# Layer 3's feed-forward weights prepared inside layer 2's feed-forward loop

## The chip, the cores and the metric

One core of a Trainium2 chip runs the whole program. The metric is the device time of one execution in microseconds (us); less is better. Five runs of the kernel before gave a median of 2343.83 us (2341.57 to 2348.78).

## What is computed

Four layers work on x (4 batches of 256 tokens of 256 numbers), each with an attention over a context of 1601 tokens and a feed-forward part. Two pieces of the reference matter here. Layer 2's feed-forward part chooses one of 4 experts for each token; layer 3's rounds its three weight matrices to -1, 0 or 1 by the mean of their absolute values:

```python
def _L2_ffn_ref(...):                      # 4 experts, top 1
    g = jnp.einsum('td,edf->tef', x, Wg)   # D_FF = 1024
    u = jnp.einsum('td,edf->tef', x, Wu)
    y = jnp.einsum('tef,efd->ted', jax.nn.silu(g) * u, Wd)
...
def _quant_weight(w):                      # layer 3: w_gate, w_up, w_down
    scale = jnp.mean(jnp.abs(w)) + EPS
    wq = jnp.clip(jnp.round(w / scale), -1.0, 1.0)
    return (wq, scale)
```

Each of the three matrices is 256 x 1024 in float32, 1 MB. Nothing in them depends on x, so they can be prepared at any time before layer 3's first feed-forward product.

## The kernel before, in words

**Layer 2's feed-forward part** is `l2_ffn` (L988). Tokens are sorted by expert into 11 groups of 128; the sorted rows are fetched with indirect DMAs on GpSimd's queue (`f2xr`, L1134). The loop at L1183 has 44 working steps (4 chunks of the hidden width times 11 groups) and two more. In a step, TensorE makes `f2gu` of one group, turns the `f2h` of the step before, and multiplies the `f2h` of two steps before into `f2y`; ScalarE takes the silu and copies `f2hT`; VectorE multiplies into `f2h` (L1158) and adds `f2y` into `f2acc` (L1176). Steps 10 to 15 also carry one piece each of layer 3's early keys and values (`fill`, L1188), the last of which ends in a root of `ss` and in `l3_spread` (L1841): GpSimd scales `kr` (L1850) and makes the lower halves (L1901), VectorE makes the upper halves (L1900) and turns them into `kt` (L1854), SyncE sends `kt` to a buffer `kd` in DRAM. The instructions of this function are placed by a scheduler, except those that are pinned to the order in which they were written (`pin`, L165).

**Layer 3** is `l3` (L1917). Its main loop has 208 steps: 4 batches, 4 passes over the context in each, 13 steps of 128 context tokens in a pass. A step makes eight score products `s`, two exponentials `e` of 128 x 1024 on ScalarE, and, for the step before, eight products into `o`. After a pass, VectorE copies `o` to `os` (L2308); the tile `o` has one buffer, so the next pass's products into `o` wait for that copy. Keys come back from `kd` as `kf` through SyncE's queue (L2123) and GpSimd copies them to `kb` (L2132).

Everything else of layer 3 is laid into these steps as streams of pieces: `slot` (L2216) lets one piece that needs TensorE into a step, and others by their stated VectorE cost until some 2 us are full. In batch 0 the streams are the weights (`weights`, L2006), the next batches' keys (`l3_keys`), their spreading (`l3_spreads`), and the next batch's queries and values. In this loop all instructions stand in the order in which they were written, on every engine.

`weights` handles the matrices one after the other, each in two halves of 128 x 1024: two loads on GpSimd's queue, two sums of absolute values on VectorE (`wsum`), a product with a matrix of ones on TensorE that adds them over the partitions, three small operations for the scale, and three VectorE operations for each half (multiply and round by adding a large number; subtract it and cut above; cut below into bfloat16). Layer 3's feed-forward pieces (`half`, L2209) start in batch 1 and wait until all three are there.

Of the kernel before, what the change touches and what calls it, by code (L numbers as in the profile page):

```python
# [11 lines left out]
F32 = mybir.dt.float32  # L12
BF16 = mybir.dt.bfloat16
# [11 lines left out]
P = 128  # L25
# [3 lines left out]
D = 256  # L29
# [68 lines left out]
class Kernel:  # L98
# [889 lines left out]
    def l2_ffn(self, other):  # L988
# [13 lines left out]
        with ExitStack() as es:  # L1002
# [142 lines left out]
            def brought(n):  # L1145
                tp = ps.tile([P, 2, P], F32, name="f2tpx", tag="tp")
                for k in range(2):
                    nc.tensor.transpose(tp[:, k, :], xr[n][:, k * P : (k + 1) * P], self.ident)
                self.evac(xsT[:, n], tp)
                expert.append(nc.tensor.value_load(ei[:, n : n + 1], min_val=0, max_val=E2 - 1))  # L1150
# [28 lines left out]

            work = [(c, n) for c in range(NC) for n in range(NS)]  # L1180
            hs, hTs = {}, {}
            brought(0)
            for s in range(len(work) + 2):  # L1183
                if s < len(work):
                    hs[s] = gated(*work[s])
                    if s + 1 < NS:
                        brought(s + 1)
                    elif s < NS + 5:  # L1188
                        fill(1)
                    elif s >= len(work) - 5:  # L1190
                        fill(1)
                if 0 <= s - 1 < len(work):
                    hTs[s - 1] = turned(hs.pop(s - 1))
                if s >= 2:
                    down(*work[s - 2], hTs.pop(s - 2))
                    c, n = work[s - 2]
                    if n == NS - 1 and c + 2 < NC:
                        chunks.append(load(c + 2))
            self.back = []
            for t in range(8):  # L1200
                if t % 4 == 0:
# [546 lines left out]
    def values3(self, pool):  # L1748
# [6 lines left out]
            self.nc.vector.memset(t[:, :, n:], 1.0)  # L1755
        return va

    def l3_begin(self, b, st):
        st["kr"] = self.a3.tile([P, NM, D], F32, name="kr3")
        st["ss"] = self.a3.tile([P, NM * NH3], F32, name="ss3")  # L1760
        st["kd"] = self.dram.tile([16, 32, MP], F32, name=f"kd3{b}")
        st["made"] = 0
# [154 lines left out]
    def l3(self, first):  # L1917
# [10 lines left out]
        with ExitStack() as es:  # L1928
# [5 lines left out]
            ps_o = es.enter_context(tc.tile_pool(name="a3o", bufs=1, space=PSUM))  # L1934
            idb = self.idb
            self.va3.append(self.values3(self.late3))
            wq, ws = {}, {}

            def bank():
                return ps.tile([P, 512], F32, name="b3", tag="tp")  # L1940
# [25 lines left out]
            def queries(b, st, fill=lambda n: None):  # L1966
# [35 lines left out]
                fill(2)  # L2002
                st["qr"] = qr
                yield 0.0

            def weights():  # L2006

                for name, n in (("l3_wg", 2), ("l3_wu", 2), ("l3_wd", 8)):
                    v = i[name].rearrange("(k p) e -> p k e", p=P)
                    w = []  # L2010
                    for c in range(2):
                        w.append(two.tile([P, I3], F32, name="wf3", tag="g3"))
                        nc.gpsimd.dma_start(
                            w[c].rearrange("p (k e) -> p k e", k=n // 2), v[:, c * n // 2 : (c + 1) * n // 2]
                        )
                    for _ in range(2):
                        yield 0.0
                    sm = self.small.tile([P, 2], F32, name="wsum")
                    for c in range(2):
                        yield 1.2  # L2020
                        nc.vector.tensor_reduce(sm[:, c : c + 1], w[c], AX.X, ALU.add, apply_absolute_value=True)
                    yield 0.0
                    yield True
                    tot = bank()[:, 0:2]
                    self.mm(tot, self.ones, sm, True, True)
                    s = one.tile([P, 1], F32, name=name + "s")
                    r = self.small.tile([P, 1], F32, name="wrec")
                    nc.vector.tensor_reduce(s, tot, AX.X, ALU.add)
                    nc.vector.tensor_scalar(s, s, 1.0 / (I3 * D), 1e-5, ALU.mult, ALU.add)
                    nc.vector.reciprocal(r, s)  # L2030
                    wb = one.tile([P, n, 2048 // n], BF16, name=name + "b")
                    wr = wb.rearrange("p k e -> p (k e)")
                    for c in range(2):
                        yield 0.8
                        nc.vector.tensor_scalar(w[c], w[c], r, RND, ALU.mult, ALU.add)
                        yield 0.7
                        nc.vector.tensor_scalar(w[c], w[c], RND, 1.0, ALU.subtract, ALU.min)
                        yield 0.7
                        nc.vector.tensor_scalar(wr[:, c * I3 : (c + 1) * I3], w[c], -1.0, None, ALU.max)
                    wq[name], ws[name] = wb, s  # L2040
                    yield 0.0

            def scale_of(v, name):

# [162 lines left out]
                states[b]["xn"] = normed(b, rs[:, b, :])  # L2207

            def half(b, q):  # L2209
                while len(wq) < 3 or "xn" not in states[b]:  # L2210
                    yield 0.0
                yield 0.7
                yield from ffn(b, q, states[b]["xn"], lambda dt: ps.tile(
                    [P, 512 if dt is F32 else 1024], dt, name="b3", tag="tp"))
# [47 lines left out]
            self.clock3 = 0  # L2262
            for at, (b, g, c) in enumerate(order):
                if g + c == 0:
                    streams = [t for t in streams if t.left] if b else [Stream(weights(), 3)]
                    st = states[b + 1] if b + 1 < B else None
                    if b + 1 < B:
                        every.n, every.share = 0, K3[b]
                        if b == 0:
                            streams += [every, Stream(self.l3_spreads(states), 1)]  # L2270
                if c == 0:
                    o = ps_o.tile([P, 2 * S], F32, name="o3")
                    now_q = q
                k, m0 = k1, PARTS[c][0]
                for m in range(*PARTS[c]):
                    e = scores(k, now_q, (m, m0))
                    if m == m0 and at + 1 < len(order):
                        k1 = exact(*kf)
                        if at + 2 < len(order):
                            b1, g1, c1 = order[at + 2]  # L2280
                            while "sent" not in states[b1]:
                                slot(streams, True, 2.0)
                            kf = keys(b1, g1, *PARTS[c1])
                    free = True
                    if m == 2 and done is not None:
                        close(*done)
                        done = None
                        free = False
                    if m == 7 and (g < 3 or b + 1 < B):
                        b1, g1 = (b, g + 1) if g < 3 else (b + 1, 0)  # L2290
                        while "qr" not in states[b1]:
                            slot(streams, True, 2.0)
                        ask = asked(b1, g1)
                        q = next(ask)
                    if m == 9 and (g < 3 or b + 1 < B):
                        next(ask)
                        free = False
                    if g * NM + m == 1 and b + 1 < B:
                        asking, valuing = Stream(ahead(b + 1, st), 2), Stream(self.l3_values(b + 1, st), 13 if b else 2)
                        streams += [asking, valuing]  # L2300
                    if g * NM + m == 3 and b:
                        streams += [Stream(behind(b - 1), 1), *(Stream(half(b - 1, n), 7) for n in range(2))]
                    slot(streams, free, 1.7 - (0.6 if m == 0 else 0.0) - (0.0 if free else 0.9))
                    if last is not None:
                        values(*last)
                        if last[4] == NM - 1:
                            os = one.tile([P, 2 * S], F32, name="os3")
                            nc.vector.tensor_copy(os, last[1])  # L2308
                            done = (last[5], os, last[3])
                    last = (e, o, states[b]["va"], g, m, b)  # L2310
                if (g, c) == (3, len(PARTS) - 1):
                    due = streams if b + 1 == B else [asking, valuing]
                    while any(t.left for t in due):
                        slot(streams, True, 2.0)
# [19 lines left out]
    def run(self):  # L2334
# [21 lines left out]
            self.l1_ffn(weights)  # L2356
        self.l2_xattn()
        with ExitStack() as es:
            self.l3_open(es)
            first = {}  # L2360
            kv = self.l3_early(0, first, lambda: True)
            self.l2_ffn(kv)
            self.l3(first)
# [124 lines left out]
```

## Time and profile before

| what | value |
|---|---|
| median of five runs | 2343.83 us |
| the profiled execution | 2350.39 us |
| its span | 2348.7 us |
| TensorE busy | 2244.7 us (96%) |
| VectorE busy | 1478.0 us (63%) |
| ScalarE busy | 1277.9 us (54%) |
| layer 2's feed-forward loop, first to last silu | 1693.5 to 1826.7 us |
| layer 3's steps, first to last exponential | from 1855.9 us to about 2313 us |

PE is TensorE's matrix products, DVE is VectorE, ACT is ScalarE, POOL is GpSimd, SP is SyncE. Times in views of the trace are microseconds from the start of the span. L117 and L77 are the lines of two helpers through which many operations are recorded, so tiles are named beside them. The chain of waits follows the work that ended last back from step to step. The clock is the share of TensorE's full clock that was granted.

### The profile page before, as it was taken

The page shows a single profiled execution, that of the slowest core. Times are in us where ns is not written, and L with a number is a line of the kernel's source. Part 1 is how long each engine was busy: PE and PEld are TensorE (multiplying, and loading weights), DVE is VectorE, ACT ScalarE, POOL GpSimd, SP SyncE. Part 2 cuts the span into 40 slices and gives each one's busy share as a digit, 9 for nine tenths or more (in the row PEclk, how much of TensorE's full clock was granted, in tenths as well). Part 3 has the DMA queues.
Part 4 walks back from the last instruction along what each step waited for, and adds up shares of the span by engine and source line. Part 5 has one row for each costly group of instructions (what it writes and reads, how often), then busy time and mean ns, then how long its engine had stood idle before and what let it go on. Part 6 is the DMA issues. An engine that isn't in the chain of part 4 may idle for free.

```text
span 2348.7 us, 42217 instructions
## 1 busy us (share of the span) xinstructions
PE 2244.7 (96%) x14322; PEld 1383.7 (59%) x14335; DVE 1478.0 (63%) x3553; ACT 1277.9 (54%) x2877; POOL 951.6 (41%) x1707
## 2 busy tenths in 40 slices
PE   8989999999989999999999999999899989999996
PEld 5677978867745565556565555656666533443332
DVE  5543645943567777777777777777344574757344
ACT  3334546633665555554455555553232587888994
POOL 2014655512445455445554455544120354334220
PEclk9989999989999999999999999999899999999998
DMA  7165687733721111111111111100543453434320
GB/s 271 42 187 166 185 155 211 259 97 108 229 80 39 45 52 52 52 52 52 52 35 51 43 52 52 52 10 1 213 137 108 142 144 101 101 94 107 82 64 17
DMA packets 156078, 234.47 MB, mean 100 GB/s; under 512 B 33929, under 2 KB 122761, under 8 KB 154666
## 3 DMA queue, kind: packets, MB, share of 16 engines
q1 hardware_dynamic: 138998, 190.07, 26.1%
q0 software_dynamic: 11280, 31.60, 6.0%
q10 hardware_dynamic: 5588, 10.09, 1.4%
q8 instruction: 117, 1.92, 0.3%
q14 instruction: 95, 0.78, 0.1%
HBM read 169.94 MB, written 61.74 MB: 99 GB/s over the span
## 4 chain that ended last, share of the span: by engine, by line
PE 76%; DVE 8%; DMA 5%; issue 4%; ACT 3%; POOL 3%; SPq 1%; ACTq 0%; POOLq 0%; DVEq 0%
PE o L117 18%; PE s L117 17%; PE o L77 6%; PE b L77 3%; PE f2gu L117 3%; PE s L77 3%; PE f1gu L117 3%; PE f0gu L117 2%; PE acc L117 2%; PE tpq L117 2%; PE av L117 2%; PE fill L1307 2%; DMA f0xr<-f0xd,f0src 2%; PE f0y L117 2%; PE f2y L117 1%
## 5 line engine op out<-in xcount | busy, mean ns | idle before, releaser
L1572 ACT ACTIVATE p<-s,nmsm 128x448 f32<-128x448 f32 (+2 forms) x512 | 324.3, 638 | 369.8 <-DVE nmsm L1567 313.4
L117 PE MATMUL o<-pT,va 128*128 128x256 f32 (+2 forms) x1920 | 434.1, 379 | 3.0 <-DVE pT L1613 2.8
L117 PE MATMUL s<-kT,qT 128*32 128x448 f32 (+2 forms) x4096 | 424.2, 551 | 4.2 <-ACT p L1572 4.2
L77 ACT ACTIVATE e<-s 128x1024 f32<-128x1024 f32 (+1 forms) x416 | 392.4, 1042 | 58.1 <-PE s L77 56.9
L117 PEld LDWEIGHTS o<-pT,va 128*128 128x128 f32 (+1 forms) x1920 | 346.7, 191 | 127.6 <-issue 75.4
L1607 POOL TENSOR_SCALAR p<-p,rm 128x448 f32<-128x448 f32 (+2 forms) x512 | 319.5, 645 | 6.3
L1567 DVE TENSOR_REDUCE nmsm<-s 128x1 f32<-128x448 f32 (+4 forms) x384 | 293.5, 784 | 4.4
L1613 DVE STREAM_TRANSPOSE pT<-p 128x448 f32<-128x448 f32 (+4 forms) x384 | 278.1, 780 | 10.7 <-POOL p L1607 10.7
L117 PEld LDWEIGHTS s<-kT,qT 128*32 128x32 f32 x4096 | 121.7, 110 | 250.5 <-issue 214.1
L77 PE MATMUL o<-e,va 128*32 128x512 f32 x1656 | 247.8, 616 | 12.7 <-DVE os L77 10.8
L1600 POOL TENSOR_TENSOR rm<-em,tot 32x8 f32<-32x8 f32 x256 | 49.9, 195 | 336.1 <-DVE tot L1597 303.8
L1564 DVE TENSOR_TENSOR s<-s,mask 128x64 f32<-128x64 f32 (+4 forms) x384 | 92.7, 260 | 129.0 <-PE s L117 82.9
L77 PEld LDWEIGHTS s<-qb,kb 32*128 32x128 f32 (+1 forms) x1664 | 65.9, 182 | 182.9 <-issue 145.1
L522 POOL DMA_INDIRECT f0xr<-f0xd,f0src x95 | 91.6, 964 | 60.9 <-PE f0tph L579 49.5
L1307 PE MATMUL fill<-wkc_early,ctxT 128*128 128x256 f32 (+1 forms) x444 | 109.5, 398 | 6.9 <-ACT va_early L1315 4.6
L77 PE MATMUL s<-qb,kb 32*128 32x256 f32 (+1 forms) x1664 | 112.0, 333 | 3.1 <-ACT e L77 1.8
L77 POOL CAST kb<-kf 128x384 fp32r<-128x384 f32 (+1 forms) x126 | 64.9, 544 | 102.6 <-PE s L77 61.6
L1572 ACT ACTIVATION_READ_ACCUMULATOR p<-s,nmsm 128x1 f32 x512 | 100.6, 196 | 0.0
L1307 PEld LDWEIGHTS fill<-wkc_early,ctxT 128*128 128x128 f32 (+1 forms) x444 | 86.2, 198 | 22.8 <-ACT va_early L1315 5.8
L77 PEld LDWEIGHTS o<-e,va 128*32 128x32 f32 x1656 | 40.8, 109 | 74.9 <-issue 37.3
L117 PE MATMUL f2gu<-f2wgu,f2xsT 128*128 x176 | 84.1, 602 | 0.8 <-issue 0.5
L630 POOL DMA_INDIRECT f0yt<-f0yd,f0slot x64 | 68.2, 1066 | 35.7 <-DMA kd<-kT_early 16.5
(579 smaller groups left out, 3678.7 us busy)
## 6 DMA issues: line engine op xcount, KB each, us to landing
kf<-kd SPq DMA_DIRECT2D x384, 48.0 KB
vd<-va_early SPq DMA_DIRECT2D x96, 128.0 KB
kd<-kT_early SPq DMA_DIRECT2D x48, 256.0 KB
kT<-kd SPq DMA_DIRECT2D x16, 768.0 KB
va<-vd SPq DMA_DIRECT2D x16, 768.0 KB
kd<-kt SPq DMA_DIRECT2D x96, 128.0 KB
f0yd<-f0ys SPq DMA_DIRECT2D x95, 128.0 KB
ctxT<-in_ctxT SPq DMA_DIRECT2D x5, 1664.0 KB
```

Source lines behind the costliest of these rows:

```text
L77: ins = f(*a, **kw)
L117: self.ordered(self.nc.tensor.matmul(out, lhsT, rhs, start=start, stop=stop, **kw))
L522: nc.gpsimd.indirect_dma_start(out=t, out_offset=None, in_=xd[:, :], in_offset=bass.IndirectOffsetOnAxis(ap=src[:, n : n + 1], axis=0),)
L630: nc.gpsimd.indirect_dma_start(out=yt, out_offset=None, in_=yd[:, :], in_offset=bass.IndirectOffsetOnAxis(ap=slot[:, t, r : r + 1], axis=0),)
L1307: ins = nc.tensor.matmul(tp[:rows, t, :], ctxT[u // NKV2][:, k, c0 : c0 + rows], w[u % NKV2][:, k, :], start=k == 0, stop=k == 1,)
L1564: nc.vector.tensor_tensor(sv, sv, mask[:, e0:e1, : nt - CT, :].rearrange("p n t i -> p n (t i)"), ALU.add)
L1567: nc.vector.tensor_reduce(ms[:, 0, e0:e1], s[:, n0:n1, : nt * 32], AX.X, ALU.max, negate=True)
L1572: nc.scalar.activation(p[:, n, : nt * 32], s[:, n, : nt * 32], AF.Exp, bias=ms[:, 0, e : e + 1], accum_out=ms[:, 1, e : e + 1],)
L1600: nc.gpsimd.tensor_tensor(r[32 * a : 32 * a + 32], e[:, a], tot, ALU.mult)
L1607: nc.gpsimd.tensor_scalar(p[:, n, : nt * 32], p[:, n, : nt * 32], r[:, e : e + 1], 1.0, ALU.mult, ALU.mult)
L1613: self.pin(nc.vector.transpose(pT[:, 2 * c + n0 : 2 * c + n1, :nt, :].rearrange("p n t i -> p n (t i)"), p[:, n0:n1, : nt * 32],))
```

## The change

A new generator `l3_weights` does what `weights` did, with tiles of its own, and layer 2's loop takes one piece of it at the end of each step from step 6 on. A piece is one sum, the product with its small operations, the first rounding operation, or the second and third together; three steps pass between the loads of a matrix and its first sum. The VectorE operations are pinned; the loads and the products are not. The stream `weights` leaves layer 3, and `half` waits no more for it.

```diff
@@ l2_ffn
             work = [(c, n) for c in range(NC) for n in range(NS)]
             hs, hTs = {}, {}
+            wf = es.enter_context(tc.tile_pool(name="f2wf", bufs=2))
+            small = self.l3_weights(wf, self.take)
             brought(0)
             for s in range(len(work) + 2):
...
+                if s >= 6:
+                    next(small, None)
+            for _ in small:
+                pass
@@ Kernel
+    def l3_weights(self, pool, bank):
+        nc = self.nc
+        self.wb3, self.ws3 = {}, {}
+        self.w3 = self.es3.enter_context(self.tc.tile_pool(name="w3", bufs=1, side="right"))
+        for name, n in (("l3_wg", 2), ("l3_wu", 2), ("l3_wd", 8)):
+            v = self.i[name].rearrange("(k p) e -> p k e", p=P)
+            w = []
+            for c in range(2):
+                w.append(pool.tile([P, I3], F32, name="wf3", bufs=2))
+                nc.gpsimd.dma_start(w[c].rearrange("p (k e) -> p k e", k=n // 2), v[:, c * n // 2 : (c + 1) * n // 2])
+            for _ in range(3):
+                yield
+            sm = self.small.tile([P, 2], F32, name="wsum")
+            for c in range(2):
+                self.pin(nc.vector.tensor_reduce(sm[:, c : c + 1], w[c], AX.X, ALU.add, apply_absolute_value=True))
+                yield
+            tot = bank()[:, 0:2]
+            self.ordered(nc.tensor.matmul(tot, self.ones, sm, start=True, stop=True))
+            s = self.ws3[name] = self.w3.tile([P, 1], F32, name=name + "s")
+            r = self.small.tile([P, 1], F32, name="wrec")
+            self.pin(nc.vector.tensor_reduce(s, tot, AX.X, ALU.add))
+            self.pin(nc.vector.tensor_scalar(s, s, 1.0 / (I3 * D), 1e-5, ALU.mult, ALU.add))
+            self.pin(nc.vector.reciprocal(r, s))
+            wb = self.wb3[name] = self.w3.tile([P, n, 2048 // n], BF16, name=name + "b")
+            wr = wb.rearrange("p k e -> p (k e)")
+            for c in range(2):
+                yield
+                self.pin(nc.vector.tensor_scalar(w[c], w[c], r, RND, ALU.mult, ALU.add))
+                yield
+                self.pin(nc.vector.tensor_scalar(w[c], w[c], RND, 1.0, ALU.subtract, ALU.min))
+                self.pin(nc.vector.tensor_scalar(wr[:, c * I3 : (c + 1) * I3], w[c], -1.0, None, ALU.max))
@@ l3
-            wq, ws = {}, {}
+            wq, ws = self.wb3, self.ws3
...
-            def weights():
...
             def half(b, q):
-                while len(wq) < 3 or "xn" not in states[b]:
+                while "xn" not in states[b]:
...
-                    streams = [t for t in streams if t.left] if b else [Stream(weights(), 3)]
+                    streams = [t for t in streams if t.left] if b else []
@@ run
         with ExitStack() as es:
+            self.es3 = es
             self.l3_open(es)
```

More of the change, by code (lines that the diff above doesn't have):

```diff
@@ L2004, in queries @@
                 yield 0.0
-            def weights():
[L2008 to L2041, printed above, removed]
             def scale_of(v, name):
```

## The prediction

> **What bounds the kernel now.** I read the busy shares by slice first, then layer 3 cut into its passes, the chain of waits at the places where a pass is too long, and at last the rows of the moved work. The first columns are 40 slices of 58.7 us.
>
> ```profile
> PE   8989999999989999999999999999899989999996
> DVE  5543645943567777777777777777344574757344
> ACT  3334546633665555554455555553232587888994
> ```
>
> TensorE is busy nearly everywhere. VectorE stands at 3 to 4 tenths in layer 2's feed-forward part (slices 29 to 31, counted from 1) and at 5 and 7 where layer 3 begins (slices 32 and 33). Next come windows whose edges I set where the exponentials of a pass begin: four passes of batch 0, then the first of batch 1. Columns: length, busy time and count of PE, weight loads, DVE, ACT and POOL, then the granted clock.
>
> ```profile
> 1856.00:1885.00 29.00, 27.99 (x218) 11.31 (x218) 23.57 (x62) 23.91 (x26) 11.14 (x18) 0.88 0.63 204
> 1885.00:1920.00 35.00, 28.83 (x234) 10.72 (x232) 27.51 (x60) 25.15 (x29) 17.64 (x23) 0.90 0.55 133
> 1920.00:1947.00 27.00, 25.91 (x227) 9.68 (x224) 11.24 (x25) 24.58 (x28) 11.39 (x21) 1.00 0.61 147
> 1947.00:1978.00 31.00, 30.07 (x252) 13.27 (x256) 15.89 (x42) 24.96 (x26) 11.66 (x18) 1.00 0.28 71
> 1978.00:2015.00 37.00, 33.09 (x264) 14.49 (x262) 23.28 (x57) 25.18 (x27) 16.83 (x24) 0.91 0.54 136
> ```
>
> Where nothing disturbs it a step lasts 1.84 us (18 exponentials take 16.52 us in the timeline), a pass 23.9. The second and the fifth window are 11 and 13 us too long, PE is idle 6 and 4 us in them, and the clock is below 1. The chain of waits between the first two passes names the cause (start, length, work):
>
> ```profile
> 1884.34 1.69 DVE xn L77 x2
> 1886.03 1.48 DVE l_wgb L77
> 1887.52 1.16 DVE kt L77
> 1888.67 0.64 DVE wf L77
> 1889.31 0.60 DVE xT L77
> 1889.90 0.60 DVE wf L77
> 1890.51 0.61 DVE os L77
> ```
>
> VectorE is behind with its pieces, `os` stands at the end of its queue, and the next pass's products into `o` wait for `os`. Three of these rows are weights.
>
> **What the change moves.**
>
> ```profile
> L77 DVE TENSOR_REDUCE wsum<-wf x6: 1189/1210/1219, 1867.6 to 1934.5; 128x1 f32<-128x1024 f32 x6
> L77 DVE TENSOR_SCALAR wf<-wf,wrec x6: 705/743/1077, 1880.2 to 1974.8; 128x1024 f32<-128x1024 f32 x6
> L77 DVE TENSOR_SCALAR wf<-wf x6: 677/683/686, 1883.4 to 1979.1; 128x1024 f32<-128x1024 f32 x6
> L77 DVE TENSOR_SCALAR l_wgb<-wf x2: 684/1123/1562, 1886.0 to 1891.4; 128x1024 bf16<-128x1024 f32 x2
> L77 POOL DMA_DIRECT2D wf<-in_l_wg x2: 563/578/593, 1857.5 to 1858.1; - x2
> ```
>
> (ns: least, median, most.) On VectorE the `wf` tiles cost 22.1 us in 24 operations, and nine small ones of some 0.16 us make 23.5. On TensorE three products with ones cost 0.26 plus 0.19 for the weights. On GpSimd six load issues cost 3.9 us. All of it goes from layer 3 into layer 2's loop; the total on each engine stays the same.
>
> *Gain 1, passes 1 and 2 (64 us).* In the changed order of VectorE, with this trace's mean durations, the work ahead of the first `os` falls from 29.0 to 25.3 us and from there to the second from 25.0 to 17.5: 54.0 against 42.8. So VectorE is no longer the limit, and ScalarE's floor of 47.8 us (26 steps) is. Above it remain what the weights don't cause: the slow steps at the start (two of 4.7 and 3.1 us with the clock at half: 4), a few query and key products (1), and perhaps half of the boundary stall (3), since other pieces move up into the freed room. 56 against 64: **8 us**. Ends: 2.7, the three rows of the chain alone; 11.2, all of the VectorE work.
>
> *Gain 2, passes 3 and 4 (58 us).* The 13 key products of batch 2 begin in pass 3 instead of late in it, since the spreading is through earlier. Each makes a step 2.5 us (PE `s` 0.44, `b` 1.06, `o` 1.00) wherever it stands: twice 23.9, plus 13 times 0.66, is 56.4. **1 us**; ends -2 and 3.
>
> *Gain 3, the boundary to batch 1 (37 us).* There the chain runs POOL `sq`, DVE `ss`, DVE `l_wdb`, DVE `os`, PE `o` (1.93 us at half clock instead of 1.00). In the changed order only short root operations precede that `os`. **3 us**; ends 0.6, the `l_wdb` row alone, and 6, the whole stall with the slow clock behind it.
>
> A rule on the clock bears here: the trace shows half clock granted right after each of these stalls, about 3.4 us at a time (0.90 over 35 us is the same loss). [...]
>
> *Cost 1, the start of layer 2's loop.* In the changed order GpSimd issues the first load before the gathers `f2xr` that TensorE waits for (PE is idle from 1684.4 to 1689.2). The issue is 0.6 us, and its 512 KB share the software queue with the gathers: 1.2 us at the 426 GB/s that the DMA view shows at most. They overlap in part; **1.2 us**, ends 0.5 and 2.5.
>
> *Cost 2, three products with ones* stand on TensorE, which has no gap in that loop (69.8 of 70 us busy from 1760). 0.45 each: **1.3 us**; ends 0.6 (weight loads hidden) and 1.4. In layer 3 they are within gains 1 and 2.
>
> *Cost 3, the wait in the middle of the loop.* Today `kt` on VectorE waits for GpSimd's `kr` and `half` (POOL fills the chain from 1747.2 to 1757.0 except 0.8 us), `f2h` waits behind `kt`, and two steps are 1.2 and 2.0 us late. In the changed order GpSimd does six `kr` (6.6 us) and a load issue before the first `half`, where it did three, so the first `kt` comes 4 us later; but one more `f2h` stands ahead of it, and a step is 2.8 us. A sum of 1.2 stands ahead of the next `f2h`. With the 1.7 us for which VectorE sits idle before each `f2h` as slack, I count 3.5 us of stall instead of 3.2: **0.3 us**; ends -3.2 (gone) and 4.
>
> *Cost 4, the pieces themselves.* The largest is 0.68 + 0.7 us in the 1.7 us of idle time of a step: **0**. That cover fails where an operation of 0.7 takes 1.6, as the `l_wgb` row has it while GpSimd works; then a step is some 0.6 late, and three or four such make the other end, 2.
>
> [...]
>
> *At nothing:* the four memsets of `va` (0.9 us) move behind the loop, where VectorE waits from 1830 to 1836 for `f2yt`; without that cover, 1 us. `kt` is sent to `kd` some steps later, on a queue that finished 20 us ahead of layer 3.
>
> **Sum:** 8 + 1 + 3 - 1.2 - 1.3 - 0.3 = 9.2 us less. The profiled execution took 2350.39 us (span 2348.7), 6.6 above the median of 2343.83 and near the highest run; the gain is a difference within it, so I take it off the median: **2334.6 us**.
>
> **The rivals.**
>
> *More comes free* (0.20). All three gains near their upper ends, since each stall brings slow clock with it: 11 + 2 + 5 - 2 = 16 less, 2328. For it: window two has 6 us of idle PE. Against it: the freed room fills with other VectorE pieces.
>
> *Hidden anyway* (0.16). The passes are held by GpSimd and by the way of the keys through `kd`, so that only the rows on the chains go: 2.7 + 0 + 0.6 - 1.2 = 2 less, 2342. For it: POOL `sq` and `half` stand on the chains. That the weights keep work in layer 3 is excluded by the order: no piece of them is left there.
>
> *Slower: the loop waits for the loads* (0.08). The sums stand in VectorE's fixed order ahead of the next `f2h`, and each waits for a load that GpSimd issues late, behind `kr`, and that shares the engines with 3.3 MB of `ctx` (DMA share 0.65 around 1750). The one landing that the trace gives is 5.3 us; by my count the second half of l3_wu is due 8.6 us after its issue, and 1.6 of slack follows. From a landing of 10 us on every further microsecond stops TensorE. It takes 15 in sum over the four late halves to turn 9 faster into 5 slower: about 2349.
>
> **How the numbers follow.** Forecast 0.56, more 0.20, hidden 0.16, slower 0.08. A measurement of this kernel tells 0.2% (4.7 us) from no change: faster 0.76, same 0.16, slower 0.08. The range reaches from just beyond the larger gain (2326) over the hidden case to 2344; what is left out is slower, or an even larger gain.
>
> **What would show it.** Pass 2 at 27 to 30 us instead of 35 and the first of batch 1 at 33 to 35 shows gains 1 and 3; passes 1 and 2 still over 62 would make them wrong. First silu of layer 2 later by 1 to 2 us: cost 1. Steps late around 1750 by more than 5 us: cost 3. VectorE waiting in that loop for a DMA into `wf`: the slower rival.

## The result, and the profile after

The changed kernel takes 2350.95 us (median of 32 runs, 2341.79 to 2356.46), the kernel before 2344.09 us (57 runs): 1.0028 of before, 95% interval 1.0021 to 1.0034, some 6.6 us slower. The forecast was 2334.6 us. The profiled execution took 2351.48 us with a span of 2349.8 us, only 1.1 us more than that of before. That is chance in the stages ahead of the change: the products `f2st`, after which layer 2's loop starts, ended at 1684.4 us in the trace of before, at 1675.5 in this one, and at 1674.5 to 1682.7 in eight more traces of kernels that share these stages. So I compare medians, and traces only by the length of a stage.

The busy shares of the page, slices of 58.7 us as before:

```profile
PE   8989999999899999999999999999899898999996
DVE  5553646943577777877787777776355645556344
ACT  3334546633655555555554555553332677878994
```

VectorE has taken up work in slices 30 to 32 and lost it in slices 33 (7 to 4) and 35 (7 to 5): the work moved as it should. The same five passes of layer 3, edges where the exponentials of a pass begin (length; busy time of PE, weight loads, DVE, ACT, POOL; granted clock):

```profile
1852.90:1886.10 33.20, 29.67 (x232) 12.03 (x236) 25.48 (x61) 24.60 (x28) 14.71 (x20) 0.90 0.64 187
1886.10:1914.10 28.00, 25.91 (x216) 8.49 (x210) 15.93 (x45) 24.53 (x29) 12.85 (x23) 0.88 0.48 105
1914.10:1947.30 33.20, 30.95 (x251) 13.18 (x248) 8.93 (x24) 24.97 (x28) 10.60 (x19) 0.95 0.37 83
1947.30:1976.10 28.80, 26.84 (x232) 10.32 (x234) 16.56 (x36) 24.46 (x26) 16.86 (x22) 1.00 0.47 129
1976.10:2012.50 36.40, 32.48 (x255) 13.89 (x252) 21.48 (x64) 25.03 (x27) 13.36 (x24) 0.91 0.55 122
sum 159.60, PE 145.85 PEld 57.92 DVE 88.38 ACT 123.60 POOL 68.37; mean PE 29.17 PEld 11.58 DVE 17.68 ACT 24.72 POOL 13.67
```

Cut at its own edges, the kernel before has 158.90 us here, with 101.38 of VectorE work. So 13 us of that work are gone and the passes are no shorter. What VectorE does instead stands in its waits from 1853 to 1978 us (us in total, times, longest). Before:

```profile
DVE kt L77 <- POOL half L77: 3.2, 2, 2.6
DVE kt L77 <- DMA kd<-kt: 1.5, 1, 1.5
```

After:

```profile
DVE kt L77 <- POOL half L77: 9.7, 5, 4.1
DVE kt L77 <- DMA kd<-kt: 6.8, 2, 5.7
```

In sum, 4.7 us of waiting for these two became 16.5. The chain at the end of the second pass shows how that reaches TensorE (start, length, work):

```profile
1913.65 2.70 DMA kd<-kt
1916.36 0.04 DVEq L77
...
1916.89 0.45 DVE kt L77
1917.33 0.59 DVE os L77
```

`kt` has two buffers; a third `kt` waits until the send two before it has landed, and that send stood on SyncE behind eight loads of `kf` of 0.42 us each. `os` stands directly behind this `kt` on VectorE, and TensorE, which had been ready for 2.25 us, starts `o` at 1917.96. `os` needed nothing from this `kt`, and the last product into `o` had ended at 1915.28; it started at 1917.33, when `kt` ended.

In layer 2's loop GpSimd has six `kr` ahead of the first `half`:

```profile
1741.05 7.33 POOL kr L1889 x6
1748.37 0.54 POOL wf L1774
...
1748.93 1.29 POOL half L1940
...
1750.25 1.25 DVE kt L1893
```

Before there were three, and `half` began at 1750.49, 57.0 us after the first silu; here it is 62.0 us.

```profile
1747.16 3.33 POOL kr L1850 x3
1750.49 1.23 POOL half L1901
```

TensorE waits 2.24 and 1.11 us for `f2h` instead of 0.98 and 1.78, and then half clock (0.50) is granted for 3.4 us, from 1758.74 on, which the loop before does not have (windows of after, then of before; the clock is the third number from the end):

```profile
1758.00:1764.00 6.00, 5.65 (x14) 2.92 (x15) 3.88 (x11) 0.70 (x2) 0.64 (x2) 0.72 0.13 35
```

```profile
1758.00:1764.00 6.00, 4.75 (x18) 3.11 (x19) 4.46 (x11) 1.02 (x3) 1.28 (x1) 1.00 0.32 67
```

### The profile page after: what moved, and what is told of

Its sections match the earlier page's. It is cut to its first block, busy times and chain, and to the rows that moved or that the text cites. A ratio compares the mean times of both kernels' runs of the same rounds, so it can differ in the third digit from the quotient of the medians.

```text
span 2349.8 us, 42222 instructions
## 1 busy us (share of the span) xinstructions
PE 2244.6 (96%) x14322; PEld 1379.9 (59%) x14335; DVE 1476.2 (63%) x3553; ACT 1278.5 (54%) x2877; POOL 947.4 (40%) x1707
## 4 chain that ended last, share of the span: by engine, by line
PE 79%; DVE 7%; DMA 5%; issue 3%; ACT 3%; POOL 2%; SPq 1%; ACTq 0%; POOLq 0%; DVEq 0%
PE o L117 18%; PE s L117 17%; PE o L77 7%; PE b L77 4%; PE f2gu L117 3%; PE s L77 3%; PE f1gu L117 3%; PE fill L1313 2%; PE acc L117 2%; PE f0gu L117 2%; PE tpq L117 2%; PE av L117 2%; DMA f0xr<-f0xd,f0src 2%; PE s L318 2%; PE f0y L117 1%
## 5 line engine op out<-in xcount | busy, mean ns | idle before, releaser
L77 ACT ACTIVATE e<-s 128x1024 f32<-128x1024 f32 (+1 forms) x416 | 392.3, 1041 | 62.6 <-PE s L77 61.2
L117 PEld LDWEIGHTS s<-kT,qT 128*32 128x32 f32 x4096 | 121.7, 109 | 249.7 <-issue 213.1
L77 PE MATMUL o<-e,va 128*32 128x512 f32 x1656 | 250.7, 624 | 16.5 <-DVE os L77 14.6
L522 POOL DMA_INDIRECT f0xr<-f0xd,f0src x95 | 91.5, 964 | 58.8 <-PE f0tph L579 45.7
L77 PE MATMUL s<-qb,kb 32*128 32x256 f32 (+1 forms) x1664 | 112.4, 332 | 2.8 <-ACT e L77 1.8
```

The costliest lines, as they stand in the source:

```text
L77: ins = f(*a, **kw)
L117: self.ordered(self.nc.tensor.matmul(out, lhsT, rhs, start=start, stop=stop, **kw))
L522: nc.gpsimd.indirect_dma_start(out=t, out_offset=None, in_=xd[:, :], in_offset=bass.IndirectOffsetOnAxis(ap=src[:, n : n + 1], axis=0),)
```

## The experiments

My theory after the traces: in layer 3 the freed room of the steps drew other pieces forward, and these wait for GpSimd and for sends, so that a wait took the place of VectorE's backlog ahead of `os`; and layer 2's loop pays some us for the pieces. The rivals: the forecast gains are there and the loop eats them; the amount of VectorE work or of early key products does it; or layer 3 is held by GpSimd and the keys wherever the pieces stand.

All stages in one table, in us: *start*, from the last `f2st` to the first `f2tpx`; *loop*, first silu to last `f2acc`; passes 1 to 4 (batch 0), batches 1 and 2; *layer 3*, first to last exponential. Ratios are to the kernel before in the same session with 95% intervals; each rests on 5 to 12 runs of the kernel (32 of the changed one), the stages on one trace each. Those marked * ran on another chip, on which the kernel before took 2389.3 us instead of 2344 to 2345; layer 3 begins some 42 us later there (at 1897.1 us in e6_room_kept, at 1854.8 in e10_late_room).

| kernel | median | ratio | start | loop | 1 to 4 | batch 1 | batch 2 | layer 3 |
|---|---|---|---|---|---|---|---|---|
| before | 2344.09 | 1 | 3.5 | 136.7 | 122.5 | 122.4 | 113.6 | 458.0 |
| changed | 2350.95 | 1.0028 (1.0021-1.0034) | 6.0 | 140.7 | 123.2 | 124.8 | 114.7 | 462.2 |
| e1_both | 2348.88 | 1.0015 (1.0003-1.0027) | 5.4 | 139.6 | 121.7 | 122.5 | 113.6 | 457.3 |
| e2_none | 2350.62 | 1.0022 (1.0010-1.0034) | 4.8 | 137.5 | 120.5 | 124.8 | 115.0 | 460.0 |
| e3_os_act | 2341.06 | 0.9984 (0.9972-0.9995) | 5.1 | 139.8 | 115.7 | 120.5 | 112.3 | 449.7 |
| e4_late | 2348.59 | 1.0021 (1.0008-1.0034) | 5.5 | 138.1 | 120.8 | 123.6 | 114.2 | 458.1 |
| e5_before_os* | 2380.29 | 0.9960 (0.9946-0.9975) | 4.6 | 137.4 | 118.5 | 118.4 | 112.4 | 450.6 |
| e6_room_kept* | 2376.98 | 0.9954 (0.9937-0.9971) | 6.0 | 140.7 | 110.6 | 120.3 | 113.6 | 444.0 |
| e9_late_room_os* | 2378.02 | 0.9948 (0.9934-0.9961) | 5.6 | 138.1 | 112.7 | 117.4 | 112.4 | 443.8 |
| e12_late_os* | 2385.99 | 0.9980 (0.9966-0.9993) | 5.0 | 139.1 | 115.6 | 120.6 | 112.3 | 449.9 |
| e10_late_room | 2333.30 | 0.9956 (0.9943-0.9969) | 5.2 | 138.8 | 110.8 | 121.2 | 113.6 | 445.0 |
| e13_room_only | 2341.32 | 0.9993 (0.9982-1.0004) | 6.4 | 140.6 | 110.9 | 125.5 | 115.0 | 450.9 |
| e14_os_first | 2343.98 | 1.0003 (0.9992-1.0014) | 5.3 | 139.9 | 117.1 | 124.1 | 113.5 | 454.7 |
| e15_room_small | 2343.34 | 1.0000 (0.9989-1.0012) | 5.1 | 139.9 | 115.4 | 121.9 | 114.2 | 450.9 |

**Which layer loses.** One kernel has the pieces in the loop and layer 3 as before; one has layer 3 as changed and no pieces.

```diff
# e1_both, on before: l3_weights with tiles of its own, stepped in the loop
+                if s >= 6:
+                    next(small, None)
# e2_none, on the changed kernel: in the loop, and in l3_weights in place of the pieces
-                if s >= 6:
+                if s >= 38:
...
+            self.pin(nc.vector.memset(s, 0.5))
+            self.pin(nc.vector.memset(wb, 1.0))
```

> The kernel before, with the changed kernel's pieces also run in layer 2's loop; what they make is not used, and layer 3 keeps its own stream of weights. Theory (a wait takes the place of the backlog, in both layers): the loop's price alone is the 2.4 us at its start and the 3.9 us inside it that the two traces show, so about 6 us slower than before, and layer 3 from its first to its last exponential stays at 458 us. Rival (the pieces are free in the loop and the whole loss arises in layer 3): within 2 us of before.

> The changed kernel without the pieces: the rounded weights are constants that six memsets write, so layer 3's feed-forward output is not the reference's. Only layer 3's loss of the stream is left. Theory: layer 3 gains nothing from losing 23.5 us of VectorE work, since os now stands behind kt pieces that wait for the sends and for GpSimd: first to last exponential 460 to 463 us as in the changed kernel, the time 0 to 4 us above before. Rival (the forecast's gains are there, and layer 2 eats them): first to last exponential 446 to 450 us, the time 8 to 12 us below before.

Both lose: 3.5 us (0.7 to 6.3) with the pieces alone, 5.2 us (2.3 to 8.0, where 0 to 4 were expected) with the lost stream alone. Layer 3 is at 457.3 us in the first and at 460.0 in the second; of the second's 5.2 us the stages show 2.3 there (457.7 is the mean of the two kernels with the stream), and the rest lies within the interval. The rival of e2_none falls: layer 2 eats no gain of layer 3. That of e1_both falls by the stages, since its loop takes 139.6 us against 136.7 to 137.5 in the three kernels without the pieces; its time alone does not exclude it. The 6 us for the loop that I read from two single traces are more than the means of the stages give (4.2, below), though the interval still holds them.

**What holds the passes.**

```diff
# e3_os_act on the changed kernel, e5_before_os on before, in the loop
-                            nc.vector.tensor_copy(os, last[1])
+                            nc.scalar.copy(os, last[1])
```

> The changed kernel with the 15 copies of o to os inside layer 3's loop on ScalarE instead of VectorE. Theory (the passes are held because os stands in VectorE's order behind pieces that wait): the PE stalls ahead of o at the ends of passes (2.1, 2.3, 1.7, 3.9 and 3.2 us in the changed kernel, 13 in sum) shrink to below 1 us each, ScalarE's copies cost some 0.6 us in the passes that ScalarE bounds, so 5 to 9 us below the changed kernel. Rival (the passes are long because keys or GpSimd are late): less than 2 us.

> The kernel before with the 15 copies of o to os in layer 3's loop on ScalarE. Theory (what os waits for sets layer 3's length, and the amount of VectorE work does not): layer 3 from first to last exponential falls from 458 us to 448 to 452 us, the same within 2 us as the changed kernel has it with this edit (449.7), although the weights are still among its pieces; the time 6 to 9 us below before. Rival (VectorE's load counts as such): layer 3 stays at 454 us or more here, so that taking the weights out is worth 5 us once os is elsewhere.

With `os` off VectorE layer 3 falls to 449.7 us with the weights moved and to 450.6 with the weights still in it. TensorE's waits for `os` from 1853 to 1978 us, in the changed kernel and then in e3_os_act:

```profile
PE o L77 <- DVE os L77: 6.0, 3, 2.2
```

```profile
PE o L77 <- ACT os L77: 3.1, 3, 1.5
```

So what stands ahead of `os` sets the length in both kernels, and 23.5 us of VectorE work more or less make 1 us once it does not. The longest wait left in e3_os_act is 1.5 us, where below 1 was expected. Its `kt` still wait 16.5 us for `half` and for `kd`, as in the changed kernel: these waits cost that much only as long as `os` stands behind them. The time of e3_os_act is 3.8 us below before (0.9984), or 10 below the changed kernel, a little more than the 5 to 9 expected; e5_before_os is 9 us below before (0.9960), where 6 to 9 were expected.

**Does the freed room draw the wrong pieces forward?** A stream in layer 3 that repeats the old `yield`s of `weights` and issues nothing:

```diff
# e6_room_kept, on the changed kernel
+            def hold():
+                for _ in range(3):
...
+                    for c in range(2):
+                        yield 1.2
+                    yield 0.0
+                    yield True
+                    for c in range(2):
+                        yield 0.8
+                        yield 0.7
+                        yield 0.7
+                    yield 0.0
-                    streams = [t for t in streams if t.left] if b else []
+                    streams = [t for t in streams if t.left] if b else [Stream(hold(), 3)]
# e13_room_only: the same without yield True
# e15_room_small, on the changed kernel: the room 1.7 of a step is 1.1 in batch 0
```

> The changed kernel with a stream in layer 3 that takes the weights' places in the steps, with their stated costs and the place on TensorE, and issues nothing, so that every other piece of layer 3 stands where it stands in the kernel before. Theory (the freed room drew other pieces forward: keys' halves and kt into the end of each pass, two sends in a row on SyncE, so that os waits behind them): layer 3 from first to last exponential falls from 462 us (458 to 462 in the three kernels without the stream) to 446 to 452 us, passes 1 and 2 to 55 to 58 us, and the time 8 to 12 us below the changed kernel. Rival (the passes are held by GpSimd and the way of the keys wherever the pieces stand): layer 3 at 456 us or more, within 3 us of the changed kernel.

> The changed kernel with a stream in layer 3 that takes only the weights' stated VectorE costs and not their three places on TensorE. Theory (what is drawn into the freed VectorE room does the harm): layer 3 at 444 to 449 us, as with both. Rival (the early key products, which take the freed places on TensorE, do it): 455 us or more.

> The changed kernel with the room of a step in batch 0 cut from 1.7 to 1.1, which slows all pieces there alike instead of holding the weights' places. Theory (the pieces come too densely for GpSimd, the sends and VectorE's order): passes 1 to 4 together shorter than the changed kernel's 123.3 us by 5 to 10, layer 3 at 448 to 456 us; what is put off may lengthen batch 1. Rival (which pieces meet matters, and not how dense they are): 458 us or more.

e6_room_kept is the deciding run: it issues the same instructions as the changed kernel in another order, and layer 3 falls from 462.2 to 444.0 us, passes 1 and 2 to 54.1, passes 3 and 4 to 56.6. It ran on the other chip; e10_late_room, with the same stream, has 445.0 us where the kernel before takes 2344. How long TensorE stands still ahead of `o` at the ends of the four passes of batch 0 goes with it: 7.5 us in sum before, 9.9 in the changed kernel, 3.7 in e6_room_kept and in e10_late_room, 3.1 in e3_os_act.

The waits of `kt` do not vanish with the order kept: 10.0 us in some 125 us from the start of layer 3, against 4.7 before and 16.5 in the changed kernel. At the end of the second pass of e6_room_kept a `kt` waits 3.29 us ahead of `os`, but it is done before `o` is, and `os` then waits 0.39 us for `o`. So what counts is whether a waiting piece stands ahead of `os` when `o` is ready, and not the sum of the waits. The kept order also leaves 9 us less VectorE work in the five passes (79.4 against 88.4 us), so this run alone does not separate which pieces meet from how many there are; e15_room_small does so in part.

In e13_room_only the stated VectorE costs alone shorten batch 0 as much (110.9 us), but leave batches 1 and 2 as long as in the changed kernel (125.5 and 115.0): there it is the three places on TensorE that count, by a way that I did not follow up. 444 to 449 us were expected for layer 3 and 450.9 measured, so both rivals hold a part of the truth. A smaller room (e15_room_small) shortens batch 0 by 8 us, as expected: thinner helps, the old order helps more.

**How far back in the queue.**

```diff
# e14_os_first, on the changed kernel
+                    ended = last is not None and last[4] == NM - 1
+                    if ended:
+                        values(*last)
+                        os = one.tile([P, 2 * S], F32, name="os3")
+                        nc.vector.tensor_copy(os, last[1])
                     slot(streams, free, ...)
```

> The changed kernel with the products of a pass's last step and the copy to os written ahead of the pieces of that step instead of behind them. Theory: only the pieces of earlier steps stand ahead of os on VectorE, so a part of the stalls ahead of o at the ends of passes (13 us in sum in the changed kernel) goes: layer 3 at 450 to 456 us. If it goes wholly (449.7 us, as with os on ScalarE), the pieces of that one step are what os waits for; if it stays at 458 to 462 us, those of the steps before. Rival (os is late because o itself is late): 458 to 462 us with os waiting for TensorE.

454.7 us lies in the expected range. In batch 0 `os` now starts 2.2 us behind the last product into `o`, summed over the four passes, where the changed kernel has 10.1: nearly all that stood ahead of `os` were pieces of that last step. Yet only about half of the time comes back (5.4 of the 10.4 us between 460.1, the mean of the three kernels without the stream, and 449.7), and pass 1 is as long as in the changed kernel (33.1 us). VectorE now waits 6.7 us for `o` in the first 125 us, and the pieces behind `os` come later; whether that is what the rest goes to is not shown.

**The start of the pieces, and the best of both.**

```diff
# e4_late, e10_late_room (with hold), e12_late_os, e9_late_room_os
-                if s >= 6:
+                if s >= 18:
```

> The changed kernel with the pieces from step 18 on instead of step 6. GpSimd's order of kr and half then is that of the kernel before; the first load of l3_wg still stands ahead of the gathers. Theory (in the changed loop six kr and a load stand on GpSimd ahead of the first half, so kt and every f2h behind it come later): the loop's stall around 1745 us falls from 6.5 back to about 3.2 us, 3 us below the changed kernel; the start of the loop and layer 3 stay. Rival (the loop is longer for the three products and the pieces themselves): no more than 1 us below.

> The changed kernel with two edits: the pieces from step 18 on and os on ScalarE. Theory: the late start takes 2 to 3 us off the changed kernel with os on ScalarE (2341.1 us), layer 3 stays at 448 to 451 us; 6 to 8 us below before. Rival (the start does not matter): 2340 to 2342 us.

> The changed kernel with three edits: the pieces from step 18 on, their room in layer 3 left empty, and os on ScalarE. Theory: the loop is 1 us longer than before, layer 3 at 444 to 449 us (the floor of e3 less what the early kt cost in its first pass), 9 to 13 us below before. Rival (os on ScalarE takes all that the room gives): the same as the next kernel within 1 us.

> The changed kernel with two edits: the pieces from step 18 on, and the stream that keeps the weights' places in layer 3 and issues nothing. Theory: the loop (first silu to last sum) 138 us instead of 140.7, the price of the products alone; layer 3 at 444 us from first to last exponential, as with the kept places alone; 0.994 to 0.995 of before, 2 to 3 us below the kernel with the kept places alone. Rival (the start of the pieces does not matter): 0.9954 of before again.

With the late start GpSimd has three `kr` ahead of the first `half` again, the two waits for `f2h` are 0.97 and 1.78 us, no half clock follows, and the loop is 138.1 to 139.1 us long instead of 139.6 to 140.7. In the times the 2 us cannot be told (0.9956 against 0.9954, 0.9980 against 0.9984, 1.0021 against 1.0028): expected of e12 were 6 to 8 us below before, and it is 4.8 below. `os` on ScalarE on top of the kept places gives nothing (443.8 us), while the kept places on top of `os` on ScalarE do (0.9948 in e9_late_room_os against 0.9980 in e12_late_os, intervals apart), so the rival of e9_late_room_os falls.

e10_late_room beats both kernels: 2333.3 us, 10.3 us below before. Its five passes, 146.00 us instead of 159.60:

```profile
1854.80:1882.70 27.90, 26.79 (x217) 10.47 (x218) 21.66 (x56) 24.17 (x27) 12.74 (x18) 0.94 0.55 177
1882.70:1909.00 26.30, 25.77 (x228) 9.63 (x229) 15.02 (x45) 24.71 (x30) 12.13 (x19) 1.00 0.58 134
1909.00:1934.90 25.90, 25.46 (x227) 9.64 (x224) 8.15 (x22) 24.29 (x28) 9.68 (x20) 1.00 0.52 114
1934.90:1965.60 30.70, 30.38 (x258) 13.39 (x261) 13.19 (x36) 24.93 (x26) 10.79 (x18) 1.00 0.29 72
1965.60:2000.80 35.20, 32.27 (x255) 13.90 (x248) 21.55 (x54) 25.02 (x27) 16.47 (x24) 0.90 0.55 142
```

Passes 2 to 4 run at full clock, and TensorE idles under 0.6 us in each.

## Why the prediction was wrong, step by step

*Gain 1* is the step that failed, and with it the forecast. "VectorE is no longer the limit" was drawn from its work between two `os` (54.0 to 42.8 us). The work did fall: from the start of layer 3 to the second `os` VectorE is busy 52.7 us before and 41.7 in the changed kernel. But I had the new order before me and summed only durations. The `kt` that moved up wait for `half` and for `kd`, 16.5 us in sum instead of 4.7, and where such a wait stands ahead of `os` it takes the place of the work that went: TensorE stands still ahead of `o` for 9.9 us in batch 0 instead of 7.5. Passes 1 and 2 came to 61.2 us (58.8 and 59.5 in e2_none and e4_late) instead of 56; with the stream in layer 3 they take 64.1 before and 61.1 in e1_both. So some 3 of the 8 us came. The forecast's own sign for gain 1, pass 2 at 27 to 30 us, even came true (28.0), while pass 1 grew from 29.3 to 33.1. With the order kept the two are 54.1: the 8 us and more were there, and the fill took them.

*Gain 2* (1 us) became a loss of about 2, which is no more than the spread of the two traces with the stream: passes 3 and 4 take 61.3 to 62.1 us without it, 58.4 and 60.6 with it in before and e1_both. It was not the key products, which I had priced: with the VectorE room alone kept, the two passes take 56.9. *Gain 3* (3 us) was nothing: 36.4 us both times, now with `ss` roots and a `kt` that waited 4.1 us ahead of `os`; it is 34.3 and 35.2 with the order kept, but 35.2 in e4_late as well, without it. Batches 1 and 2, on which I put no term behind that, lose another 2.4 and 1.1 us. In sum layer 3 is 2.4 us longer (460.1 against 457.7, the means of three and two kernels) where 12 less were forecast; with the order kept it is 13 less.

*Cost 1* was right: the start takes 5.5 us on average in the eleven kernels with the load there (5.0 to 6.4), 4.3 in the three without (3.5 to 4.8): 1.2. *Cost 2* was mis-sized: each product lengthens a step by 0.22 us (3.02 instead of 2.80), 0.7 in sum instead of 1.3, since its weight loads (0.19 us each) run while the products ahead of it are still busy: the first one of `l3_wd` starts at 1785.34 in the changed kernel, with the last of the `f2y` ahead of it busy until 1785.72. *Cost 3* was right in kind and wrong in size: the first `kt` is 5.0 us later (I had 4), but with the half clock behind the longer stall the loop loses 2.3 us and not 0.3 (140.2, the mean of the seven early loops, less 137.2, that of the three without pieces, less the products). It is 2.8 in the three kernels where two more waits follow (the changed one, e6_room_kept, e13_room_only) and 1.9 in the other four. *Cost 4* and the memsets at nothing hold: behind the stall all steps without a product stay at 2.80.

Start, loop and layer 3 together, 1.2 + 3.0 + 2.4, make the measured loss of 6.6 us; that they do so to a tenth is luck, as layer 3 alone differs by 4 us among the three kernels without the stream. For e10_late_room they are 1.2 + 1.3 - 13 = -10.5.

Of the rivals, *hidden anyway* named the two things that the `kt` wait for, GpSimd and the way through `kd`, but as a floor under the passes that caps the gain at 2 us. With the order kept layer 3 is 13 us shorter, so they are no floor; they matter where `os` stands behind them. *The loop waits for the loads* is out: VectorE waits for no load of `wf` there.

## What to carry to other kernels

Where a filler lays pieces into steps by their stated cost, taking a stream out is a change of order for all the others: read in the new order what stands directly ahead of the instruction that the bound engine waits for, and what each of these waits for itself, not only how long they take. If a freed room makes things worse, keep it empty first; that one run separates the work that went from what filled its room. And start added work where no chain over several engines runs already.

## What the runs showed of the hardware

The stalls cost more here than their idle time where half clock (0.50 in the trace's record) follows: in the kernel before TensorE waits 3.09 us for `os` until 1891.16, and 0.50 is granted from 1890.93 to 1894.35. The eight products of a step into `o` take 1.87 to 1.94 us at half clock instead of 1.00. In e1_both, e3_os_act, e14_os_first and e15_room_small TensorE stands still for 2.23 or 2.24 us in the middle of layer 2's loop; within 0.5 us of the end of that wait half clock is granted for 3.4 us. In the changed kernel, e6_room_kept and e13_room_only a standstill as long is not followed by it at once; the half clock comes some 6.4 us later, after two more of 1.11 and 0.58 us. The loop before, with 0.98 and 1.78 us within 6 us, keeps the full clock there, and so do the four kernels with the late start. So in this loop no half clock followed 1.78 us, it followed 2.23 or 2.24 us at once in four kernels of seven, and length alone does not decide; what else does is not shown.

From layer 2's first silu to layer 3's last exponential the clock is halved for 34.2 us in the changed kernel, 20.5 before and 11.6 in e10_late_room, by the trace's record of the granted clock.
